# A second source-sorted table for 12 more pairs, and the first pairs dealt out in lots over layer one

## The chip, the cores and the metric

The kernel runs on one core of a Trainium2 chip. The metric is the device time of one launch in microseconds. The core has five engines that run their own instruction streams in order: TensorE (PE, with its weight loads shown as PEld), VectorE (DVE), ScalarE (ACT), GpSimd (POOL) and SyncE (SP). DMAs are issued by SP, ACT and POOL. POOL issues the indirect ones, in which every row has an address of its own.

## The reference, cut to what matters

Three layers of a relational graph network over N = 6250 nodes of D = 256 features and E = 100000 edges with R = 3 relations, all float32:

```python
ew = edge_attr @ edge_w + edge_b                      # (E, 256), the same in all layers
for l in range(3):
    msg = relu(x[src] * ew)                           # a row of x per edge
    out = 0
    for i in range(3):                                # relation i
        h = segment_sum(msg * (edge_type == i), dst) * inv_cnt[i]
        out = out + h @ weights[l, i]
    x = x + relu(out + x @ roots[l] + biases[l])
return layernorm(x0 + x)
```

The edges come sorted by `dst`, and `dst` is drawn as 6250 u², so that the low nodes have by far the most edges: the first 7168 edges all end in the first 40 nodes.

## The kernel before, in words

**Pairs and steps.** Edges are taken 128 at a time, one to a partition, and two such tiles are a pair: 391 pairs of 256 edges. A quad is two pairs (four tiles, 128x1024 elements). In every layer a list `order` says in which order the pairs are worked, and the loop over `it` is software-pipelined around it: at step `it` PE reduces pair `order[it]`, DVE multiplies (`weigh`) the quad of pair `order[it+3]`, PE makes the edge weights of `order[it+5]` (layer one; later layers load them back from `ew_all`), and POOL gathers pair `order[it+9]`. The steps only fix the order of each engine's own instructions; in time the engines run apart as far as data and buffers allow. Gathered rows sit in `xs`, which has 8 quad buffers, so that POOL can be some 16 pairs ahead of the reduction.

**A pair's work.** `gather_pair` (L1300) issues two indirect DMAs on POOL, 128 rows of x each. `weigh` multiplies a quad by its edge weights on DVE (L813) and applies relu on ACT (L814). `one_hot` builds four 128x120 selection tiles on DVE (L827: 3 relations by a window of 40 nodes). `reduce` multiplies rows by selections on PE into `h_p` (L844 or L852), and `add` puts the 40-node window of a span of pairs into the ring `acc` on DVE (L884, or L873 for the place of the first 40 nodes, which needs no address). When a block `c` of 128 nodes is complete (step `starts[c]`), `node_mul` multiplies it by the relation weights on PE (L913), `node_end` adds up on DVE (L944, L947) and SP stores the block to `x_mid` in DRAM (L950) for the next layer's gathers; in layer three DVE also does the layer norm of the block (L953 to L965, L1015). Blocks 1 to 48 end in order, 4 to 16 steps apart; block 0, where the most edges end, ends last.

**The zone.** The first Z = 28 pairs all end in the first 40 nodes. In layer one they are gathered like the others, 28 pairs in one run at steps 104 to 131, and `scatter` (L708) also writes each of their edge-weight rows with an indirect DMA on POOL into `zone_table` in DRAM, sorted by source: one scatter behind each gather, four to a quad. The place of each row in the table is counted out beforehand in layer one (`sort_begin`, `sort_hot`, `sort_count`, `sort_end`), and `sort_clear` blanks the table (L599). In layers two and three these 28 pairs are not gathered. Instead 25 *lots* of 2 pairs (one per 256 source nodes) stand in the order, one every 12 pairs (`ZONE_EVERY`): SP loads 512 table rows (L725), and since each of a lot's four tiles holds edges from one known half-block of 64 sources, the rows of x are made on chip: PE spreads the row numbers over the partitions (`seed_ew`, L753), DVE compares them with the partition number (`choose`, L769, 128x256), PE multiplies that by `x_all` in SBUF (`expand`, L777), and DVE weighs the result (L813, tile `zone`). No indirect DMA is issued for a lot.

**The end of a layer.** Pairs 51 down to 28 end in the first 128 nodes and come last in every layer; with them block 0 is complete. `gather_early` then issues the next layer's first 6 pairs (12 indirect DMAs from `x_mid`, tile index `src_e`), which read all blocks but block 0; what they lack of block 0 is added on chip (`complete`). It stands `SOON` = 3 steps before the end of the order. After that the gathers need block 0 in `x_mid`.

Of the kernel before, what the change touches and what calls it, by code (L numbers as in the profile page):

```python
# [442 lines left out]
def ordered_path(ctx, tc, x, attr_laid, A, weights, roots, biases, edge_w, edge_b, out, src, src_i, seg, place_i, consts, x_root,  # L443
# [6 lines left out]
    nc = tc.nc  # L450
# [12 lines left out]
    Z = zone_of(N, E)  # L463
    ZU = first_zone(N, E)
    slots = 2 * (ZU + 2 * -(-NT // 2) - ZU) * P
# [97 lines left out]

    zt = 2 * Z
# [14 lines left out]

    def sort_begin():  # L580
# [8 lines left out]
        nc.vector.tensor_scalar(slot_i, mine, P // 2 - 1, None, op0=ALU.bitwise_and)  # L589
        nc.vector.tensor_copy(meta[:, :, 0], seg[:, :zt])  # L590
# [11 lines left out]
    def sort_hot(g):  # L602
        hots[g] = early_pool.tile([P, 4, WK], BF, name="sort_hot")
        for i in range(4):
            t = 4 * g + i
            nc.vector.tensor_scalar(hots[g][:, i, :], iota_w[:, :, :WIN], slot_f[:, t:t + 1], None, op0=ALU.is_equal)
            if t == 0:
# [13 lines left out]
    def sort_end():  # L621
        most_p = o_pool.tile([P, 2, D], F32, name="o_p")
        crowd = early_pool.tile([P, 2], F32, name="crowd")
        nc.vector.tensor_reduce(crowd[:, 0:1], rank, AX.X, ALU.max)
        nc.vector.scalar_tensor_tensor(slot_f, slot_f, float(P), rank, op0=ALU.mult, op1=ALU.add)
# [37 lines left out]
    def layer(l, r_sb, b_sb, ats, early, pools):  # L663
# [5 lines left out]
        steps = len(order)  # L669
        taken, turns, added, banks = stages(N, E, share, l)  # L670
# [8 lines left out]
        r_next, ats_next, early_next = (None, None), {}, {}  # L679
        seen, h_bank, ew_ss, zone, hot, row_in, waiting = [0], {}, {}, {}, {}, {}, []  # L680
# [23 lines left out]
        def scatter():  # L704
            if waiting:
                there, q, k, i = waiting.pop(0)
# [60 lines left out]
        def choose(q):  # L767
            hot[q] = late_pool.tile([P, 2, P], F32, name="hot", bufs=2)
            nc.vector.tensor_scalar(hot[q].rearrange("p i e -> p (i e)"), ew_ps[q][:, 0, 0, :], half_i, None,  # L769
                                    op0=ALU.is_equal)  # L770

        def expand(q):
            c = 2 * (q - ZU // 2)
# [6 lines left out]
        def make_ew(q):  # L780

            n = len(pairs_of(q))
            at = ats[2 * q // GROUP, 2 * q < Z][:, q % (GROUP // 2), :]
# [85 lines left out]
        def add(span):  # L869
            u = span[0]  # L870
            if u < Z or u >= ZU:
# [115 lines left out]
        if l > 0:  # L987
            for p, u in enumerate(order):
                if u >= ZU:
                    assert all(p - 5 < starts[c] for c in (u - ZU, u - ZU + 1 - 2 * (u % 2)) if 0 < c < NT)  # L990
        for it in range(-11, max(starts) + 8):
            def pair(k):
# [3 lines left out]
            if l < L - 1 and 0 <= it + SOON - steps < FIRST:  # L996
                gather_early(it + SOON - steps)
# [5 lines left out]
            if l == 0 and pair(AHEAD) is not None and (pair(AHEAD) // GROUP, pair(AHEAD) < Z) not in ats:  # L1003
                ats[pair(AHEAD) // GROUP, pair(AHEAD) < Z] = load_at(pair(AHEAD) // GROUP)
# [80 lines left out]
            for span in add_at.get(it, ()):  # L1085
                add(span)
        return (*r_next, ats_next, early_next)
# [21 lines left out]
ROOTS = 24  # L1109
# [8 lines left out]
CLEARS = 20  # L1118
CLEAR_EVERY = 4
SORT_AT = 4  # L1120
SORT_EVERY = 5
ZONE_AT = 104
ZONE_FROM = 12
ZONE_EVERY = 12
# [4 lines left out]
def zone_of(N, E):  # L1129
# [7 lines left out]
    return v  # L1137

# [33 lines left out]
def zone_pairs(N, E):  # L1172

    ZU = first_zone(N, E)
    return [(ZU + 2 * j, ZU + 2 * j + 2) for j in range(-(-N // 256))]


def spans_in(N, E, l):

    spans = spans_of(N, E)  # L1180
    return spans if l == 0 else spans[1:] + zone_pairs(N, E)
# [15 lines left out]
def order_of(N, E, l):  # L1197
# [3 lines left out]
    Z = zone_of(N, E)  # L1201
# [4 lines left out]
    if l == 0:  # L1206
        at = where(K + ZONE_AT)
        order[at:at] = range(Z - 1, -1, -1)
    else:
        for j, (u, v) in enumerate(zone_pairs(N, E)):  # L1210
# [7 lines left out]
def stages(N, E, share, l):  # L1218

    order = order_of(N, E, l)  # L1220
    Z = zone_of(N, E)
# [257 lines left out]
```

## Time and profile before

| | |
|---|---|
| median of 3 runs | 2923.25 us (2922.34 to 2927.55) |
| profiled execution, its own time | 2919.59 us |
| its span | 2917.5 us |
| layer one on POOL, up to its last gather | 1064.2 us |
| layer two on POOL, last gather to last gather | 920.4 us |
| from layer two's last gather to the end | 932.9 us |
| busy: PE, DVE, ACT, POOL | 80%, 73%, 58%, 75% |
| indirect DMAs on POOL | 2234 gathers, 56 scatters |
| mean granted TensorE clock | 0.93 |

The profiled execution lies 3.7 us (0.13%) under the median. Busy times are of the engine itself; what its sequencer needs to issue a DMA is not in them, so that an engine that issues DMAs without a pause is shown under 100%.

### The profile page before, as it was taken

The numbers are of one execution on the slowest core, as the hardware profiler recorded it, in microseconds if no ns is written. First come the engines' busy times: TensorE is split into PE (matmuls) and PEld (weight loads), VectorE is DVE, ScalarE is ACT, GpSimd is POOL, SyncE is SP. The second block draws the span as 40 slices with busy tenths as digits, with TensorE's granted clock in tenths as the row PEclk, the third lists the DMA queues.
The fourth block names the chain that finished last, engine by engine and source line by source line (L and its number), as shares of the span: only waits on it lengthen the run. The fifth ranks groups of instructions, "written<-read, shape, count | busy, mean of one in ns | idle before, by whom it ended". The sixth has DMA issues, their size and how long they took to land.

```text
span 2917.5 us, 42955 instructions
## 1 busy us (share of the span) xinstructions
PE 2346.3 (80%) x12885; PEld 1799.7 (62%) x12885; DVE 2125.3 (73%) x5375; ACT 1694.0 (58%) x2153; POOL 2179.8 (75%) x2300
## 2 busy tenths in 40 slices
PE   5799768989999996778888888777677887877776
PEld 2456535667666765556667676665455666766665
DVE  7787424777777866666778788776577778988987
ACT  5678636877777765555555455444455554544554
POOL 7777777777777767777777777777777777777775
PEclk9999968999999998898999999989899998999999
DMA  7888536767767668677777777767777777777775
GB/s 236 307 306 289 175 123 202 226 219 234 236 219 240 228 225 264 222 231 233 241 228 235 228 240 241 238 215 246 223 242 230 233 247 231 244 241 231 249 246 174
DMA packets 275051, 679.64 MB, mean 233 GB/s; under 512 B 50986, under 2 KB 124732, under 8 KB 274812
## 3 DMA queue, kind: packets, MB, share of 16 engines
q1 hardware_dynamic: 157456, 368.21, 36.2%
q0 software_dynamic: 109920, 300.36, 34.2%
q10 hardware_dynamic: 7436, 8.24, 0.9%
q8 instruction: 106, 1.74, 0.2%
q14 instruction: 133, 1.09, 0.1%
HBM read 541.38 MB, written 135.23 MB: 232 GB/s over the span
## 4 chain that ended last, share of the span: by engine, by line
PE 25%; POOL 14%; DMA 13%; issue 12%; DVE 10%; ACT 2%; DVEq 1%; SPq 0%; ACTq 0%; POOLq 0%
POOL xs L1300 14%; DMA xs<-x_mid,src_r 11%; PE h_p L852 8%; PE o_p L913 7%; PE h_p L844 4%; DVE xs L813 3%; PE ew_p L791 3%; DVE oh L827 2%; DVE acc L884 1%; DVE x_root L944 1%; PE r_p L897 1%; PE ew_p L777 1%; ACT xs L814 1%; DMA ew_s<-ew_all 1%; PE r_p L889 1%
## 5 line engine op out<-in xcount | busy, mean ns | idle before, releaser
L1300 POOL DMA_INDIRECT xs<-x_mid,src_r x1428 | 1354.8, 949 | 437.9 <-issue 372.6
L814 ACT ACTIVATE xs<-xs 128x1024 f32<-128x1024 f32 (+1 forms) x557 | 585.0, 1050 | 792.0 <-DVE xs L813 770.3
L813 DVE TENSOR_TENSOR xs<-ew_p,xs 128x1024 f32<-128x1024 f32 (+1 forms) x557 | 675.6, 1213 | 381.8 <-DMA xs<-x_mid,src_r 195.7
L1300 POOL DMA_INDIRECT xs<-in_x_dram,src_io x770 | 733.6, 953 | 238.6 <-issue 194.9
L852 PE MATMUL h_p<-oh,xs 128*128 128x120 f32 x4848 | 685.2, 288 | 148.9 <-DVE acc L884 59.0
L852 PEld LDWEIGHTS h_p<-oh,xs 128*128 128x128 f32 x4848 | 635.3, 198 | 236.1 <-issue 93.6
L844 PE MATMUL h_p<-xs,oh 128*120 128x256 f32 x2020 | 594.5, 429 | 69.1 <-issue 20.7
L827 DVE TENSOR_SCALAR oh<-iota_w,seg_o 128x120 f32<-128x120 f32 x2234 | 593.2, 327 | 0.0
L913 PE MATMUL o_p<-w_sb,acc 128*128 128x256 f32 (+1 forms) x1752 | 468.2, 406 | 66.1 <-DVE x_root L944 61.7
L844 PEld LDWEIGHTS h_p<-xs,oh 128*120 128x120 f32 x2020 | 371.3, 203 | 202.6 <-issue 69.3
L884 DVE TENSOR_TENSOR acc<-h_p,acc 128x240 f32 (+1 forms) x741 | 327.2, 442 | 146.2 <-PE o_p L913 72.1
L913 PEld LDWEIGHTS o_p<-w_sb,acc 128*128 128x128 f32 (+1 forms) x1752 | 330.7, 200 | 151.8 <-DVE x_root L944 73.3
L758 ACT ACTIVATE ew_p<-ew_s 128x1024 f32<-128x1024 f32 x364 | 368.0, 1011 | 12.4 <-DMA ew_s<-ew_all 12.4
L791 PE MATMUL ew_p<-ew_sb,at 64*128 64x512 f32 x782 | 238.3, 686 | 66.9 <-ACT ew_p L761 59.8
L742 ACT ACTIVATE keep<-ew_p 128x1024 f32<-128x1024 f32 x182 | 185.4, 1019 | 118.4 <-issue 59.4
L944 DVE SCALAR_TENSOR_TENSOR x_root<-o_p,inv,x_root 128x256 f32<-128x256 f32 (+1 forms) x438 | 210.1, 480 | 41.5 <-PE o_p L913 34.6
L761 ACT ACTIVATE ew_p<-seed 128x1024 f32<-128x1024 f32 x194 | 198.4, 1023 | 0.0
L897 PE MATMUL r_p<-r_sb,t_s 128*128 128x256 f32 x588 | 168.0, 410 | 30.1 <-ACT t_s L893 30.0
L889 PE MATMUL r_p<-ident_o,x_all 128*128 128x128 f32 x294 | 67.8, 316 | 126.4 <-DVE x_root L900 126.1
L930 ACT ACTIVATE acc<-zero_o 128x768 f32<-128x768 f32 (+1 forms) x150 | 140.3, 936 | 20.5 <-PE o_p L913 20.4
L889 PEld LDWEIGHTS r_p<-ident_o,x_all 128*128 128x128 f32 x294 | 33.5, 150 | 187.8 <-DVE x_root L900 119.2
L897 PEld LDWEIGHTS r_p<-r_sb,t_s 128*128 128x128 f32 x588 | 107.5, 200 | 56.9 <-ACT t_s L893 40.4
(168 smaller groups left out, 1815.6 us busy)
## 6 DMA issues: line engine op xcount, KB each, us to landing
ew_s<-ew_all SPq DMA_DIRECT2D x362, 512.0 KB
ew_all<-keep SPq DMA_DIRECT2D x181, 512.0 KB
zone<-zone_table SPq DMA_DIRECT2D x50, 516.0 KB
xs<-x_mid,src_r POOLq DMA_INDIRECT x1428
zone_table<-blank SPq DMA_DIRECT2D x20, 645.0 KB
at<-in_attr_laid_dram SPq DMA_DIRECT2D x50, 256.0 KB
xs<-in_x_dram,src_io POOLq DMA_INDIRECT x770
x_mid<-x_all SPq DMA_DIRECT2D x96, 128.0 KB
```

The costliest lines, as they stand in the source:

```text
L758: nc.scalar.activation(ew_ps[q][:, :n], ew_ss[q][:, :n], AF.Copy)
L791: nc.tensor.matmul(ew_ps[q][:, k].rearrange("p i d -> p (i d)"), at[half, :], ew_sb[half].rearrange("p i d -> p (i d)"), start=False, stop ...
L813: nc.vector.tensor_mul(there, ew_ps[q][:, pairs.start:pairs.stop], there)
L814: nc.scalar.activation(there, there, AF.Relu)
L827: nc.vector.tensor_scalar(ohs[q][:, i, :], iota_w[:, :, :WIN], at, None, op0=ALU.is_equal)
L844: nc.tensor.matmul(h_p[:WK, :D], ohs[u // 2][:, t, :], rows_of(u, i), start=(i == 0 and first), stop=(i == 1 and closes(u)), skip_group_ch ...
L852: nc.tensor.matmul(h_p[:, d * WK:(d + 1) * WK], rows_of(u, i)[:, d * P:(d + 1) * P] if d < DC else full_ones, (ohs if d < DC else oh_bs)[u ...
L884: nc.vector.tensor_tensor(there, h_ps[span][:, :CH * WK].rearrange("p (c r w) -> p c r w", c=CH, r=R), there, op=ALU.add)
L897: nc.tensor.matmul(rs[c][:, 1, :], t_ss[c][:, d, :], r_sb[:, d, :], start=(d == 0), stop=(d == DC - 1))
L913: nc.tensor.matmul(o_p[:n, j, :], acc[:, d, r, slot:slot + n], w_sb[:, r * DC + d, :], start=(d == 0), stop=(d == DC - 1))
L944: nc.vector.scalar_tensor_tensor(root, o_p[:n, j, :], inv[:n, c, r:r + 1], root, op0=ALU.mult, op1=ALU.add)
L1300: nc.gpsimd.indirect_dma_start(out=xs[:, u % 2, i, :], out_offset=None, in_=x_rows[:, :], in_offset=bass.IndirectOffsetOnAxis(ap=src_i[:, ...
```

## The change

The next span, pairs 28 to 39, becomes part of the zone (`zones_end` gives 40, `zone_of` still 28). Its 12 pairs get a second part of the table, sorted by whole blocks of 128 sources, in 13 lots of 2 pairs (one per 512 sources, four tiles of one block each). Layer one keeps all gathers and issues 24 scatters more. Layers two and three lose the 12 pairs' gathers and edge-weight loads, and have 38 lots instead of 25, about one every 8 pairs; 21 of them stand behind pair 208, where 13 stood before. For a new lot PE spreads four 128x128 rows of numbers, DVE compares 128x512 elements, and PE expands with all 128 partitions. In layer one the zone's pairs no longer stand in one run: quads of them stand every 10 to 12 pairs from step 180 on, and the last six quads (pairs 11 to 0) right ahead of the last run, which is now 51 to 40. The table has 29696 rows instead of 19968 and is cleared in 30 DMAs instead of 20; the sort takes 20 groups instead of 14. The attribute load of a zone quad is one of its own (`load_one_at`). `gather_early` moves: `soon` is 3 after layer one as before, and -2 after layer two, 5 steps later, since block 48 starts at step 424 of 427 there (before: 398 of 413). `x_root` has 22 buffers instead of 24.

```diff
+    soon = min(SOON, steps - starts[NT - 1] - 5)
...
         def seed_ew(q):
...
+            if 2 * q >= Z2U:
+                for i in range(4):
+                    nc.tensor.matmul(ew_ps[q][:, 0].rearrange("p i d -> p (i d)")[:, i * P:(i + 1) * P],
+                                     row_in[q].rearrange("p k i -> p (k i)")[:, i:i + 1].to_broadcast([P, P]), ident_b,
+                                     start=(i == 0), stop=(i == 3), skip_group_check=True)
+                return
...
         def choose(q):
...
+            if 2 * q >= Z2U:
+                hot[q] = late_pool.tile([P, 4, P], F32, name="hot_4")
+                nc.vector.tensor_scalar(hot[q].rearrange("p i e -> p (i e)"), ew_ps[q][:, 0].rearrange("p i d -> p (i d)"),
+                                        node_i[:, 0:1], None, op0=ALU.is_equal)
+                return
...
         def expand(q):
...
+            if 2 * q >= Z2U:
+                c = 4 * (q - Z2U // 2)
+                for i in range(4):
+                    nc.tensor.matmul(ew_ps[q][:, i // 2, i % 2, :], hot[q][:, i, :], x_all[:, min(c + i, NT - 1), :],
+                                     start=(i % 2 == 0), stop=(i % 2 == 1), skip_group_check=True)
+                return
...
         def add(span):
-            u = span[0]
-            if u < Z or u >= ZU:
+            u = span[0] if span[0] < Z2U else Z1
+            if u < Z1 or u >= ZU:
...
-            if l < L - 1 and 0 <= it + SOON - steps < FIRST:
-                gather_early(it + SOON - steps)
+            if l < L - 1 and 0 <= it + soon - steps < FIRST:
+                gather_early(it + soon - steps)
...
-ROOTS = 24
+ROOTS = 22
...
-CLEARS = 20
+CLEARS = 30
...
-SORT_EVERY = 5
-ZONE_AT = 104
+SORT_EVERY = 6
+ZONE_AT = 168
+ZONE_SPACE = 11
+ZONE_LAST = 6
 ZONE_FROM = 12
-ZONE_EVERY = 12
+ZONE_EVERY = 8
...
+def zones_end(N, E):
+
+    return spans_of(N, E)[1][1]
...
     if l == 0:
-        at = where(K + ZONE_AT)
-        order[at:at] = range(Z - 1, -1, -1)
+        for j, u in enumerate(range(Z - 2, -1, -2)):
+            at = where(K + ZONE_AT + ZONE_SPACE * j) if K + ZONE_AT + ZONE_SPACE * j < U - 2 else order.index(U - 1) + 1 + 2 * j
+            if u < 2 * ZONE_LAST:
+                at = order.index(last - 1)
+            order[at:at] = (u + 1, u)
```

**POOL, layer one.** The program's order on POOL from the first gathers of layer one on; `zone_table<-keep,slot_i` is a scatter, `xs<-in_x_dram` a gather. Before:

```order
L1300 DMA xs<-in_x_dram,src_io 128x256 x225
L708 DMA zone_table<-keep,slot_i 19968x258
L1300 DMA xs<-in_x_dram,src_io 128x256
L708 DMA zone_table<-keep,slot_i 19968x258
L1300 DMA xs<-in_x_dram,src_io 128x256
```

Now:

```order
L1360 DMA xs<-in_x_dram,src_io 128x256 x353
L727 DMA zone_table<-keep,slot_i 29696x258
L1360 DMA xs<-in_x_dram,src_io 128x256
L727 DMA zone_table<-keep,slot_i 29696x258
L1360 DMA xs<-in_x_dram,src_io 128x256
L727 DMA zone_table<-keep,slot_i 29696x258
L1360 DMA xs<-in_x_dram,src_io 128x256
L727 DMA zone_table<-keep,slot_i 29696x258
L1360 DMA xs<-in_x_dram,src_io 128x256 x25
```

Before, 56 scatters and gathers alternate in one stretch behind the 225th gather of this row; now groups of four scatters come from the 353rd on, with 21 to 25 gathers between them, and the last six groups stand together near the end of the layer.

**DVE, the end of layer two.** The program's order on DVE from layer two's last products (`xs<-ew_p` 128x256 x2) to layer three's first. The operands `o_p,inv,x_root` are a node block's sums, `x_all<-x_root` ends the block (106 partitions: block 48; the one with `r_p` in it: block 0), and `xs<-o_p` is `complete`. Before:

```order
L819 TENSOR_TENSOR xs<-ew_p,xs 128x256 x2
L877 TENSOR_LOAD place_i
L884 ISA
L884 TENSOR_TENSOR acc<-h_p,acc 128x6x40
L944 SCALAR_TENSOR_TENSOR x_root<-o_p,inv,x_root 128x256
L944 SCALAR_TENSOR_TENSOR x_root<-r_p,inv,x_root 128x256
L944 SCALAR_TENSOR_TENSOR x_root<-o_p,inv,x_root 128x256
L947 SCALAR_TENSOR_TENSOR x_all<-x_root,x_all 128x256
L808 TENSOR_TENSOR xs<-o_p,xs 128x512
```

Now:

```order
L855 TENSOR_TENSOR xs<-ew_p,xs 128x256 x2
L963 TENSOR_TENSOR acc<-acc 128x6x40
L980 SCALAR_TENSOR_TENSOR x_root<-o_p,inv,x_root 128x256 x2
L983 SCALAR_TENSOR_TENSOR x_all<-x_root,x_all 128x256
L980 SCALAR_TENSOR_TENSOR x_root<-o_p,inv,x_root 106x256
L913 TENSOR_LOAD place_i
L920 ISA
L920 TENSOR_TENSOR acc<-h_p,acc 128x6x40
L980 SCALAR_TENSOR_TENSOR x_root<-o_p,inv,x_root 106x256 x2
L983 SCALAR_TENSOR_TENSOR x_all<-x_root,x_all 106x256
L980 SCALAR_TENSOR_TENSOR x_root<-o_p,inv,x_root 128x256
L980 SCALAR_TENSOR_TENSOR x_root<-r_p,inv,x_root 128x256
```

Before, only block 0 was left behind the last products; now blocks 47 and 48 end there too, and the early gathers of layer three, which read block 48, come after it.

**DVE, a lot in layer three.** The program's order on DVE from the comparison of a lot (`hot`) to its selections (`oh<-iota_w,zone`). Before, in the first half of the layer:

```order
L769 TENSOR_SCALAR hot<-ew_p,half_i 128x256
L900 TENSOR_TENSOR x_root<-r_p,b_sb 128x256
L827 TENSOR_SCALAR oh<-iota_w,seg_o 128x120 x4
L813 TENSOR_TENSOR zone<-ew_p,zone 128x4x256
L827 TENSOR_SCALAR oh<-iota_w,zone 128x120 x4
```

Now, one of the 13 new lots, late in the layer:

```order
L795 TENSOR_SCALAR hot_24031<-ew_p,node_i 128x512
L920 ISA
L920 TENSOR_TENSOR acc<-h_p,acc 128x6x40
L863 TENSOR_SCALAR oh<-iota_w,seg_o 128x120 x4
L920 ISA
L920 TENSOR_TENSOR acc<-h_p,acc 128x6x40
L849 TENSOR_TENSOR zone<-ew_p,zone 128x4x256
L980 SCALAR_TENSOR_TENSOR x_root<-o_p,inv,x_root 128x256
L920 ISA
L920 TENSOR_TENSOR acc<-h_p,acc 128x6x40
L863 TENSOR_SCALAR oh<-iota_w,zone 128x120 x4
```

The lot's own instructions are the same but for the comparison, which is twice as wide; 26 more of them stand on DVE in layers two and three together, and one more `add` for each.

More of the change, by code (lines that the diff above doesn't have):

```diff
@@ L989, in layer @@
                 if u >= ZU:
[L990 removed]
+                    u -= u % 2
+                    blocks = range(u - ZU, u - ZU + 2) if u < Z2U else range(2 * (u - Z2U), 2 * (u - Z2U) + 4)
+                    assert all(p - 4 < starts[c] for c in blocks if 0 < c < NT), (u, p)
         for it in range(-11, max(starts) + 8):
+            it_is[0] = it
             def pair(k):
@@ L1086, in layer @@
                 add(span)
+        assert not waiting
         return (*r_next, ats_next, early_next)
```

47 lines of the change are left out of this document (35 added, 12 removed).

## The prediction

> **What bounds the kernel now.** I read the page's head, POOL's waits, and its groups by line.
>
> ```profile
> span 2917.5 us, 42955 instructions
> PE 2346.3 (80%) x12885; PEld 1799.7 (62%) x12885; DVE 2125.3 (73%) x5375; ACT 1694.0 (58%) x2153; POOL 2179.8 (75%) x2300
> POOL xs L1300 <- issue: 573.9, 1884, 0.3
> ...
> L1300 POOL DMA_INDIRECT xs<-x_mid,src_r x1428 | 1354.8, 949 | 437.9 <-issue 372.6 <-DMA xs<-x_mid,src_r 17.1 <-PE h_p L844 7.6
> L1300 POOL DMA_INDIRECT xs<-in_x_dram,src_io x770 | 733.6, 953 | 238.6 <-issue 194.9 <-DMA xs<-in_x_dram,src_io 8.2 <-ACT ew_p L761 6.5
> L708 POOL DMA_INDIRECT zone_table<-keep,slot_i x56 | 54.8, 979 | 18.0 <-issue 14.6 <-ACT keep L736 1.3 <-DMA zone_table<-keep,slot_i 0.9
> ```
>
> No engine shows over 80%, but POOL's 75% is a full engine: a gather is busy for 0.95 us and then idle for 0.30 us, nearly always on "issue", which is its own sequencer (573.9 us in 1884 pieces of 0.3). So a gather costs 1.25 us and a scatter 1.28 us, and the 2290 of them make 2290 x 1.25 = 2863 of the 2917.5 us. Whether POOL also sets the pace is told by who waits for its rows. These are DVE's waits in layer two (1500 to 1900 us), then the first and the second half of layer three (2000 to 2400, 2400 to 2850):
>
> ```profile
> DVE xs L813 <- DMA xs<-x_mid,src_r: 28.4, 15, 5.0
> ```
>
> ```profile
> DVE xs L813 <- DMA xs<-x_mid,src_r: 77.8, 30, 5.2
> ```
>
> ```profile
> DVE acc L884 <- PE o_p L913: 17.9, 11, 3.5
> DVE mv L964 <- ACT mv L959: 12.6, 13, 1.3
> DVE zone L813 <- PE ew_p L777: 11.4, 10, 2.1
> DVE x_root L944 <- PE o_p L913: 4.3, 9, 0.9
> ...
> DVE xs L813 <- DMA xs<-x_mid,src_r: 1.0, 1, 1.0
> ```
>
> Early in layer three DVE waits 77.8 of 400 us for gathered rows: POOL paces it. From 2400 us on it waits 1.0 us for them: DVE, with the PE and ACT waits of its own instructions, is the pace, and POOL runs ahead into the free buffers. Layer two lies between, with 28.4 of 400 us to spare. The stages, with PE, PEld, DVE, ACT and POOL busy, the granted clock and the DMA share (zone run of layer one, its later part, layer two, the two halves of layer three):
>
> ```profile
> 300.00:440.00 140.00, 97.67 (x380) 59.70 (x378) 49.31 (x127) 63.61 (x82) 105.83 (x109) 0.78 0.44 139
> 600.00:1000.00 400.00, 377.88 (x2400) 280.73 (x2398) 305.99 (x735) 302.20 (x361) 302.82 (x320) 0.99 0.69 228
> 1500.00:1900.00 400.00, 319.94 (x2005) 278.29 (x2006) 317.06 (x798) 203.14 (x238) 302.56 (x320) 0.94 0.74 238
> 2000.00:2400.00 400.00, 299.79 (x1369) 228.88 (x1369) 281.15 (x697) 212.92 (x296) 302.85 (x320) 0.91 0.74 241
> 2400.00:2850.00 450.00, 349.86 (x2197) 302.33 (x2196) 392.22 (x1031) 228.43 (x292) 340.90 (x359) 0.95 0.75 242
> ```
>
> In the last row DVE is busy for 392.2 of 450 us, and the waits above add 46 us: nothing is left over. So an indirect DMA saved is worth its 1.25 us in layers one and two, and nothing behind 2400 us, where only DVE's work counts.
>
> **Layer one: +30.8 us.** All its gathers stay, and 24 scatters at 0.979 + 0.30 = 1.28 us come on a POOL that has no pause: +30.8 us. The 24 more sort groups' parts on DVE and PE, the 10 clearing DMAs and the small attribute loads on SP lie beside POOL: in the zone run DVE is busy for 49 of 140 us and the DMA engines for 44%, and later DVE for 306 of 400. If that cover failed, POOL would run out of buffers; in layer one PE, busy for 378 of 400 us, would be the first to show it. Spreading the zone removes no POOL instruction.
>
> **Hand-over to layer two: -11.5 us.** POOL's rows at the end of layer one, and of layer two:
>
> ```profile
> 1063.23 0.94 POOL L1300 DMA_INDIRECT xs<-in_x_dram,src_io  x1 [0.30 <-issue]
> 1073.05 0.95 POOL L1300 DMA_INDIRECT xs<-x_mid,src_e  x1 [8.88 <-DMA ew_all<-keep]
> ...
> 1090.93 0.94 POOL L1300 DMA_INDIRECT xs<-x_mid,src_r  x1 [3.18 <-PE o_p L806]
> ```
>
> ```profile
> 1983.67 0.95 POOL L1300 DMA_INDIRECT xs<-x_mid,src_r  x1 [0.30 <-issue]
> 1984.92 0.95 POOL L1300 DMA_INDIRECT xs<-x_mid,src_e  x1 [0.30 <-DMA xs<-x_mid,src_r]
> ...
> 1999.94 0.94 POOL L1300 DMA_INDIRECT xs<-x_mid,src_r  x1 [0.30 <-issue]
> ```
>
> From the end of the last gather to the next layer's first full one POOL needs 1090.93 - 1064.17 = 26.8 us after layer one and 1999.94 - 1984.62 = 15.3 us after layer two; 12 early gathers alone are 15.0. The difference is the lag of the other engines behind POOL: layer one ends PE-heavy (94%), so block 48 and block 0 are late. Now the last six zone quads stand there with their scatters, 24 x 1.28 = 31 us in which POOL is slower and PE is not asked for more, as in the zone run, where PE was at 70%. The gain lies between 0 and 11.5 us; I take 11.5, since 31 us are more than the whole lag.
>
> **Layer two: -30.0 us.** 24 gathers at 1.25 us fall away. What comes: in 400 us POOL gathers 160 pairs, which held 13.3 lots and now hold 20. A lot on DVE, by the starts of the next instruction (row_in, `hot`, product, `add`, selections):
>
> ```profile
> 2017.17 0.16 DVE L765 CAST row_in<-zone 128x4 bf16<-128x4 f32 x1
> 2017.24 1.06 DVE L827 TENSOR_SCALAR oh<-iota_w,seg_o 128x120 f32<-128x120 f32 x4
> 2018.23 1.21 DVE L813 TENSOR_TENSOR xs<-ew_p,xs 128x1024 f32<-128x1024 f32 x1
> 2019.36 0.47 DVE L769 TENSOR_SCALAR hot<-ew_p,half_i 128x256 f32<-128x256 f32 x1
> 2019.75 1.06 DVE L827 TENSOR_SCALAR oh<-iota_w,seg_o 128x120 f32<-128x120 f32 x4
> 2021.09 1.23 DVE L813 TENSOR_TENSOR zone<-ew_p,zone 128x1024 f32<-128x1024 f32 x1 [0.28 <-PE ew_p L777]
> 2022.23 0.40 DVE L884 TENSOR_TENSOR acc<-h_p,acc 128x240 f32 x1
> 2022.54 1.06 DVE L827 TENSOR_SCALAR oh<-iota_w,zone 128x120 f32<-128x120 f32 x4
> 2023.52 1.21 DVE L813 TENSOR_TENSOR xs<-ew_p,xs 128x1024 f32<-128x1024 f32 x1
> ...
> L808 DVE TENSOR_TENSOR xs<-o_p,xs 128x512 f32<-128x512 f32 x2 | 1.4, 686 | 1.0 <-PE o_p L806 1.0
> ```
>
> 0.07 + 0.39 + 1.14 + 0.31 + 0.98 = 2.9 us, and 11.4 / 10 = 1.1 us of waiting for the expansion: 4.0 us. The new comparison of 128x512 has no row; it lies between one and two of the old (0.39 to 0.78). The nearest row reads 128x512 from PSUM in 0.69 us of duration, 0.21 more than the 0.47 of `hot`, so a new lot takes 4.2 us. In the Trainium skill, the page "VectorE: DVE Perf Modes" (section "The TRN2 errata — SBUF-src ops pay a fixed extra latency per instruction") gives a PSUM read 120 cycles and one per element at 0.96 GHz, an estimate of 0.66 us for it and 0.39 for the old one; no run here shows the wide one, and by that figure the sum would be 0.4 us higher.
>
> So 6.7 lots more are 27 us per 400, against 28.4 us of waiting for rows: they fit, barely, and POOL keeps the pace. On PE the stage has 80 of 400 us idle for them.
>
> **Hand-over to layer three: +11.5 us.** Before, block 48 had long been stored when layer two's last gather was issued. Now it ends behind the layer's last `add`, and the early gathers wait for it. Rows of that place before (the last `add`, block 0's last step, its store):
>
> ```profile
> 1992.36 0.41 DVE L884 TENSOR_TENSOR acc<-h_p,acc 128x240 f32 x1 [3.42 <-PE h_p L852]
> ...
> 1996.24 0.42 DVE L947 SCALAR_TENSOR_TENSOR x_all<-x_root,x_all 128x256 f32<-128x256 f32 x1
> 1996.69 0.33 SPq L950 DMA_DIRECT2D x_mid<-x_all  x1
> ```
>
> The last `add` starts 7.7 us behind POOL's last gather; block 48 needs two sums and its last step (0.41 + 2 x 0.5), so its store goes out at about 9.5. Block 0's store at 1996.69 released gathers at 1999.94 at the latest, 3.3 us; with 2 to 3.3 us for landing the early gathers start at 11.5 to 12.8 and end 15 us later, 11.2 to 12.5 us behind the 15.3 of before. I take 11.5. On POOL everything of layer three queues behind them.
>
> **Layer three: +20.4 us.** Up to 2400 us POOL paces, and 5 lots more at 4.2 us go into 77.8 us of waiting: nothing. Behind pair 208, which is about there, 21 lots stand instead of 13, 7 of the 8 being new: 8 x 4.0 + 7 x 0.21 = +33.5 us. The last run has 6 quads fewer: 6 x (1.13 + 0.98) = -12.7, and one `add` less, -0.3. The sum is +20.4 us; the 30 us of gathers that POOL saves do not show. Without the waits for expansion it would be +11.7; with twice these, +29.
>
> **Sum.** 30.8 - 11.5 - 30.0 + 11.5 + 20.4 = +21.2 us against the profiled 2919.6 us, which lies 3.7 us under the median. On the median of 2923.25 that is 2944 us, 0.7% slower.
>
> **Rivals.**
> (a) Faster: DVE sheds its waits, so that POOL paces layer three to its end. Then its 24 gathers count too, and the sum is 21.2 - 20.4 - 30 = -29 us, 2894. For this the 46 us of waits behind 2400 us would have to go, since the last row of the stages leaves DVE no other room and it gets 12 us of its own work more. Nothing in the trace speaks for that.
> (b) PE runs at a higher clock. In the trace the clock was 0.78 where PE was busy for 70%, 0.99 at 94%, and 0.95 in the DVE-paced stage at 78%. With the lots' work there the stage might reach 0.99: 350 us of PE become 336, and if all 14 us come off DVE's waits the sum is +7 us, 2930. In the Trainium skill, the page "TensorE: Matmul & The Clock Gate" (section "What's actually happening") has the throttled state as the default that activity lifts; by that rule more lots pay for part of themselves, and the trace's stages agree in direction (0.78 against 0.99).
> (c) Layer two falls behind as layer one did. A lot on PE (reduction, expansion, spread numbers, 25 lots):
>
> ```profile
> L844 PE MATMUL h_p<-zone,oh 128*120 128x256 f32 x200 | 52.0, 394 | 6.6 <-DVE acc L884 4.0 <-DMA ew_s<-ew_all 2.0 <-PE h_p L852 0.6
> L777 PE MATMUL ew_p<-x_all,hot 64*128 64x256 f32 x200 | 32.0, 441 | 5.5 <-DVE hot L769 5.5
> L753 PE MATMUL ew_p<-ident_b,row_in 128*64 128x128 bf16 x100 | 8.1, 244 | 0.7 <-DVE row_in L765 0.7
> ```
>
> That is 92.1 / 25 = 3.7 us; a new one expands with all 128 rows, at most as dear as the reduction, 4.5 us. 6.7 lots more take PE to some 347 of 400 us (87%) and DVE to 337 (84%) at once; layer one at 94% of PE lagged 11.5 us at its end. That would come on the hand-over, and the waits for expansion may double (+9): 2953 to 2966.
> (d) The spread zone does not shorten the hand-over to layer two: +11.5 us, 2956.
>
> **How the numbers follow.** The forecast (2930 to 2952) has 0.47, (a) 0.08, (b) 0.15, (c) and (d) together 0.30. From no change 0.2% (5.8 us) is about what a measurement of this kernel can tell. Faster: (a) and a little of (b), 0.11. Within: most of (b), 0.13. Slower: 0.76. The range leaves out (a) and the worst of (c): 2922 to 2966. Where only "slower" counts, the forecast's own bounds are the +11.7 and +29 of layer three.
>
> **What would show it.** Right: 80 scatters without pauses on POOL in layer one and its last gather some 31 us later; a hand-over near 15 us; layer two's last-to-last gather time (920.4 us) some 42 us shorter; then a pause of POOL of about 10 us ahead of the `src_e` gathers; behind layer three's middle no DVE waits for `xs`, and POOL waiting for buffers, not for issue. Wrong: DVE waiting for `xs` late in layer three (a), a clock of 0.99 there (b), or POOL idle in the middle of layer two (c).

## The result and the profile after

| | before | after |
|---|---|---|
| median of 5 runs | 2922.34 us (2919.91 to 2927.55) | 2960.64 us (2958.67 to 2966.95) |
| ratio, 95% interval | | 1.013 (1.0117 to 1.0144) |
| profiled execution, its span | 2919.59, 2917.5 us | 2958.67, 2956.9 us |

The changed kernel is 1.3% slower, 38 us where 21 were forecast. Its median lies inside the stated range (2922 to 2966 us) but above the forecast's own bounds (2930 to 2952). The page of after, its head and its gathers of layers two and three:

```profile
span 2956.9 us, 44413 instructions
PE 2431.0 (82%) x13409; PEld 1878.4 (64%) x13409; DVE 2211.6 (75%) x5620; ACT 1712.6 (58%) x2203; POOL 2157.4 (73%) x2276
...
L1360 POOL DMA_INDIRECT xs<-x_mid,src_r x1380 | 1309.5, 949 | 458.4 <-issue 362.8
```

48 gathers fewer in these layers and 24 scatters more in layer one leave POOL with 22 us less work, and PE and DVE with 85 us each more. POOL's timeline (start, duration, idle time before and what ended it) at the first scatter, at the end of layer one and at the end of layer two:

```profile
474.45 0.94 POOL L1360 DMA_INDIRECT xs<-in_x_dram,src_io  x1 [0.30 <-issue]
485.70 0.99 POOL L727 DMA_INDIRECT zone_table<-keep,slot_i  x1 [10.31 <-ACT keep L755]
...
1101.85 0.95 POOL L1360 DMA_INDIRECT xs<-in_x_dram,src_io  x1 [0.30 <-PE h_p L888]
1103.10 0.95 POOL L1360 DMA_INDIRECT xs<-x_mid,src_e  x1 [0.30 <-issue]
...
1121.18 0.95 POOL L1360 DMA_INDIRECT xs<-x_mid,src_r  x1 [3.40 <-PE r_p L842]
...
1984.26 0.94 POOL L1360 DMA_INDIRECT xs<-x_mid,src_r  x1 [0.30 <-issue]
2001.60 0.95 POOL L1360 DMA_INDIRECT xs<-x_mid,src_e  x1 [16.40 <-PE o_p L842]
...
2016.61 0.95 POOL L1360 DMA_INDIRECT xs<-x_mid,src_r  x1 [0.30 <-issue]
```

The first scatter of the kernel before, for comparison:

```profile
318.21 0.99 POOL L708 DMA_INDIRECT zone_table<-keep,slot_i  x1 [1.25 <-ACT keep L736]
```

From these rows come the stages, cut as the prediction cut them (the end of a layer's last gather; the start of the next layer's first full gather):

| stage, us | before | after | change | predicted |
|---|---|---|---|---|
| layer one to its last gather | 1064.2 | 1102.8 | +38.6 | +30.8 |
| hand-over to layer two | 26.8 | 18.4 | -8.4 | -11.5 |
| layer two | 893.7 | 864.0 | -29.7 | -30.0 |
| hand-over to layer three | 15.3 | 31.4 | +16.1 | +11.5 |
| layer three to the end | 917.5 | 940.3 | +22.7 | +20.4 |
| span | 2917.5 | 2956.9 | +39.4 | +21.2 |

All five signs and the order of the sizes are as forecast. The largest miss is layer one. The one new wait there is the 10.31 us in the second row above (1.25 us before), which no part of the prediction mentions.

DVE's and POOL's longest waits in layer three from 2450 to 2850 us (total, times, longest), first DVE, then POOL:

```profile
DVE acc L920 <- PE o_p L949: 19.2, 10, 5.0
DVE mv L1000 <- ACT mv L995: 9.0, 10, 1.2
DVE zone L849 <- PE ew_p L813: 8.9, 6, 2.3
```

```profile
POOL xs L1360 <- issue: 81.5, 244, 1.8
POOL xs L1360 <- ACT xs L850: 14.3, 10, 5.2
POOL xs L1360 <- ACT ew_p L783: 8.5, 8, 3.8
```

DVE has no row that waits for gathered rows; POOL waits for its buffers, which come free behind DVE's products (`ACT xs`). Its last gather ends 40.0 us before the span does; before it was 22.0 us. The same stretch in the stages view, of before and of after (PE, PEld, DVE, ACT and POOL busy, granted clock, DMA share, GB/s):

```profile
2450.00:2850.00 400.00, 307.61 (x1945) 264.93 (x1944) 352.49 (x930) 204.84 (x262) 303.09 (x319) 0.97 0.75 242
```

```profile
2450.00:2850.00 400.00, 317.53 (x1926) 275.79 (x1927) 338.19 (x885) 194.38 (x247) 282.07 (x297) 0.93 0.72 232
```

Before, POOL still issued 319 DMAs in these 400 us, its full rate (one per 1.25 us). After, it issued 297: it no longer set the pace.

### The profile page after: what moved, and what is told of

It is laid out like the page before. It is cut to its first block, busy times and chain, and to the rows that moved or that the text cites. A ratio compares the mean times of both kernels' runs of the same rounds, so it can differ in the third digit from the quotient of the medians.

```text
span 2956.9 us, 44413 instructions
## 1 busy us (share of the span) xinstructions
PE 2431.0 (82%) x13409; PEld 1878.4 (64%) x13409; DVE 2211.6 (75%) x5620; ACT 1712.6 (58%) x2203; POOL 2157.4 (73%) x2276
## 5 line engine op out<-in xcount | busy, mean ns | idle before, releaser
L1360 POOL DMA_INDIRECT xs<-x_mid,src_r x1380 | 1309.5, 949 | 458.4 <-issue 362.8
L850 ACT ACTIVATE xs<-xs 128x1024 f32<-128x1024 f32 (+1 forms) x545 | 572.3, 1050 | 671.3 <-DVE xs L849 646.8
L849 DVE TENSOR_TENSOR xs<-ew_p,xs 128x1024 f32<-128x1024 f32 (+1 forms) x545 | 661.0, 1213 | 343.3 <-ACT keep L761 171.3
L880 PE MATMUL h_p<-xs,oh 128*120 128x256 f32 x1972 | 562.5, 416 | 64.2 <-issue 16.1
L880 PEld LDWEIGHTS h_p<-xs,oh 128*120 128x120 f32 x1972 | 351.1, 197 | 186.0 <-issue 41.4
L920 DVE TENSOR_TENSOR acc<-h_p,acc 128x240 f32 (+1 forms) x773 | 340.6, 441 | 149.4 <-PE o_p L949 63.7
L827 PE MATMUL ew_p<-ew_sb,at 64*128 64x512 f32 x702 | 216.4, 693 | 27.2 <-ACT ew_p L786 16.1
L850 ACT ACTIVATE zone<-zone 128x1024 f32<-128x1024 f32 x76 | 80.5, 1059 | 231.5 <-DVE zone L849 207.6
L880 PE MATMUL h_p<-zone,oh 128*120 128x256 f32 x608 | 156.4, 389 | 26.8 <-DVE acc L920 21.0
L849 DVE TENSOR_TENSOR zone<-ew_p,zone 128x1024 f32<-128x1024 f32 x76 | 92.9, 1223 | 97.0 <-PE ew_p L813 52.3
```

What stands on the lines that cost most here:

```text
L827: nc.tensor.matmul(ew_ps[q][:, k].rearrange("p i d -> p (i d)"), at[half, :], ew_sb[half].rearrange("p i d -> p (i d)"), start=False, stop ...
L849: nc.vector.tensor_mul(there, ew_ps[q][:, pairs.start:pairs.stop], there)
L850: nc.scalar.activation(there, there, AF.Relu)
L880: nc.tensor.matmul(h_p[:WK, :D], ohs[u // 2][:, t, :], rows_of(u, i), start=(i == 0 and first), stop=(i == 1 and closes(u)), skip_group_ch ...
L920: nc.vector.tensor_tensor(there, h_ps[span][:, :CH * WK].rearrange("p (c r w) -> p c r w", c=CH, r=R), there, op=ALU.add)
L1360: nc.gpsimd.indirect_dma_start(out=xs[:, u % 2, i, :], out_offset=None, in_=x_rows[:, :], in_offset=bass.IndirectOffsetOnAxis(ap=src_i[:, ...
```

## The experiments

Stages of each kernel in us, as above, from its POOL timeline, with its median and its ratio to the kernel before on the same chip. One profiled execution stands for a kernel, and equal stages scatter. Layer three without edits to it took 917 to 927 us with the old lots and 940 to 947 us with the new ones. Layer one of the kernel before took 1064.2 us and, in `nonorm_before_2`, 1071.3; that of the changed kernel took 1102.8, 1103.4 (`nonorm_after_2`) and 1101.8 (`l3_old`, which also stores six more quads there).

| kernel | median | ratio (95%) | layer one | hand-over | layer two | hand-over | layer three |
|---|---|---|---|---|---|---|---|
| `spread_only` | 2913.6 | 0.9976 (0.9967 to 0.9986) | 1063.0 | 15.3 | 894.4 | 15.5 | 927.4 |
| `second_only` | 2992.7 | 1.0237 (1.0221 to 1.0253) | 1104.8 | 47.4 | 866.3 | 32.0 | 944.5 |
| `zone_earlier` | 2973.0 | 1.0170 (1.0154 to 1.0185) | 1113.5 | 18.5 | 866.4 | 31.4 | 947.4 |
| `l3_old` | 2944.6 | 1.0077 (1.0059 to 1.0095) | 1101.8 | 20.3 | 863.3 | 31.4 | 925.9 |
| `sooner_and_free` | 2948.3 | 1.0084 (1.0069 to 1.0100) | 1101.2 | 18.6 | 864.6 | 19.0 | 946.3 |
| `spread_normact` | 2910.5 | 0.9957 (0.9943 to 0.9971) | 1067.9 | 15.3 | 894.3 | 15.4 | 915.8 |
| `nonorm_after_2` | 2912.1 | 0.9958 (0.9941 to 0.9974) | 1103.4 | 16.8 | 865.5 | 31.7 | 888.9 |
| `nonorm_before_2` | 2919.1 | 0.9983 (0.9973 to 0.9992) | 1071.3 | 27.5 | 896.8 | 15.6 | 912.2 |

### The two halves of the change

**`spread_only`**: the changed kernel without a second table, the old 28 pairs in lots.

```diff
 def zones_end(N, E):
-    return spans_of(N, E)[1][1]
+    return zone_of(N, E)
...
 def zone_pairs(N, E):
-    return [(ZU + 2 * j, ZU + 2 * j + 2) for j in range(halves + blocks)]
+    return [(ZU + 2 * j, ZU + 2 * j + 2) for j in range(halves)]
...
-CLEARS = 30
+CLEARS = 20
...
-SORT_EVERY = 6
-ZONE_AT = 168
-ZONE_SPACE = 11
+SORT_EVERY = 5
+ZONE_AT = 112
+ZONE_SPACE = 26
...
-ZONE_EVERY = 8
+ZONE_EVERY = 12
```

> The kernel before with the zone's 14 lots of two pairs spread over layer one (eight alone, six together ahead of the last 20 pairs); no second table. No DMA more or less on POOL. Theory (the hand-over to layer two is the other engines' lag behind POOL, and scatters late in the layer let them catch up): the lead of POOL over the weighing at the layer's last gather falls from 12.6 us to about 4.5 us, the hand-over from 26.8 to about 18.4 us, the time by 8 to 11 us against the kernel before: 2911 to 2914 us, ratio 0.996 to 0.997. Rival (a lag given up in layer one comes back as a stall there or in layer two): within 3 us of the kernel before.

POOL at the end of its layer one:

```profile
1062.06 0.94 POOL L1360 DMA_INDIRECT xs<-in_x_dram,src_io  x1 [0.30 <-DMA xs<-in_x_dram,src_io]
1063.30 0.94 POOL L1360 DMA_INDIRECT xs<-x_mid,src_e  x1 [0.30 <-issue]
...
1077.07 0.94 POOL L1360 DMA_INDIRECT xs<-x_mid,src_e  x1 [0.30 <-issue]
1078.31 0.95 POOL L1360 DMA_INDIRECT xs<-x_mid,src_r  x1 [0.30 <-issue]
```

No row waits: the hand-over is the 12 early gathers alone, 15.3 us instead of 26.8, less than the 18.4 expected, and the time falls by 8 us. The theory holds; rival (d) of the prediction falls. This half of the change beats the kernel before.

**`second_only`**: the changed kernel with all 40 pairs in one run.

```diff
-            at = where(K + ZONE_AT + ZONE_SPACE * j) if K + ZONE_AT + ZONE_SPACE * j < U - 2 else order.index(U - 1) + 1 + 2 * j
-            if u < 2 * ZONE_LAST:
-                at = order.index(last - 1)
+            at = where(K + ZONE_AT) + 2 * j
```

> The changed kernel with its zone of 40 pairs in one run at step 180 of layer one, instead of in lots spread over it. Theory: layer one up to its last gather stays some 31 to 39 us over that of before; after the run the lag of the other engines grows again as before, to 12 us at the last gather, so the hand-over to layer two is back near 26 us and the time is 8 us over the changed kernel, 2966 to 2971 us (ratio to the kernel before 1.016). Rival (the spreading is worth nothing): 2960 us, ratio 1.013.

It lost 32 us against the changed kernel, not 8. POOL, the end of its layer one, and DVE, the last step of block 48 (106 partitions):

```profile
1103.60 1.20 POOL L1358 DMA_INDIRECT xs<-in_x_dram,src_io  x1 [0.30 <-issue]
1137.16 0.95 POOL L1358 DMA_INDIRECT xs<-x_mid,src_e  x1 [32.37 <-ACT acc L966]
```

```profile
1131.84 0.43 DVE L983 SCALAR_TENSOR_TENSOR x_all<-x_root,x_all 106x256 f32<-106x256 f32 x1
```

Without lots behind the last edges block 48 starts at step 388 of 391, so `soon` is -2 here too, and the early gathers wait for that block, as they do after layer two: in both places the first of them starts 4.9 us behind the end of block 48's last step (here 1132.27 us), though the rows name other engines. On top of it the other engines lag by 14.8 us, where the changed kernel has 4.5. So the lots at the end do two things: they let the engines catch up, and they give block 48 time to be stored. The expectation saw the first alone.

### Layer one's stall

Lead is the time from the end of a quad's last gather on POOL to the start of its product on DVE:

| layer one, lead in us | step 96 | step 138 | step 168 | step 180 | first scatter waits |
|---|---|---|---|---|---|
| after | 12.1 | 14.4 | 19.4 | 23.8 | 10.31 |
| `second_only` | 12.6 | 13.4 | 17.7 | 22.5 | 9.00 |
| `sooner_and_free` | 13.4 | 18.9 | 16.2 | 18.7 | 5.23 |

In each row the wait is the lead at step 180 less 13.5 us, and so it is in `l3_old` (22.5 and 9.03) and `nonorm_after_2` (21.2 and 7.78). A scatter stands in POOL's order only four to five pairs, 2.5 us each, behind the last gather of its quad, and what it writes must have passed PE and ACT (`keep`): a POOL that leads by more than 13.5 us stands still there, and everything behind the scatter with it. The 13.5 us are those of step 180. In the kernel before, whose zone run stands at steps 116 to 143 (not 104 to 131), the first scatter waits 1.25 us at a lead of 12.3; in `spread_only`, at step 124, it waits 0.30 us at a lead of 11.1.

**`zone_earlier`**: first lot at step 124, sort groups every 4 pairs.

```diff
-SORT_EVERY = 6
-ZONE_AT = 168
-ZONE_SPACE = 11
+SORT_EVERY = 4
+ZONE_AT = 112
+ZONE_SPACE = 15
```

> The changed kernel with the first spread lot at step 124 of layer one instead of 180 (lots 15 pairs apart, the sort's groups every 4 pairs). At step 124 POOL leads the weighing by 13 to 15 us, at step 180 by 23.8. Theory (the 10.3 us stall at 485.70 us is the first scatter, which stands in POOL's order only ten pairs behind the gather of its rows, so that a POOL that leads by more than about 17 us waits for the kept rows): the stall falls to 0 to 3 us, layer one's last gather ends near 1093 to 1095 us instead of 1102.8, the time falls by 7 to 10 us against the changed kernel: 2950 to 2954 us. Rival (the other engines lag by as much all the same, and the stall returns at a later scatter or at the hand-over): 2960 us, no change.

A miss with the wrong sign: 12 us slower than the changed kernel. The expectation also had the distance wrong: ten pairs and 17 us, where it is four to five pairs and 13.5 us. ACT, SP and POOL there:

```profile
349.58 1.03 ACT L755 ACTIVATE keep<-ew_p 128x1024 f32<-128x1024 f32 x1 [0.70 <-PE ew_p L827]
```

```profile
345.59 0.43 SPq L613 DMA_DIRECT2D zone_table<-blank  x1
```

```profile
340.08 0.95 POOL L1360 DMA_INDIRECT xs<-in_x_dram,src_io  x1 [0.30 <-ACT keep L761]
354.26 1.00 POOL L727 DMA_INDIRECT zone_table<-keep,slot_i  x1 [13.23 <-ACT xs L850]
```

The lead at step 126 is 20.8 us, where the changed kernel has 16.0 and `spread_only`, whose sort ended at step 88, has 11.0: the denser sort made the engines lag more. By the 13.5 us of step 180 that would be a wait of 7.3 us, not of 13.23. The scatter starts 3.7 us behind the end of its `keep`; the last clearing DMA had been issued only 8.7 us before it, and probably that is what it waited for, but no row shows it. Another wait of POOL, at 103 us, took 8.43 us, where the executions with a group every 6 pairs have 2.12 to 4.48.

**`sooner_and_free`**: the sort every 5 pairs with the lots where they were; and the early gathers of layer three freed.

```diff
-SORT_EVERY = 6
+SORT_EVERY = 5
...
-        soon = min(SOON, steps - starts[NT - 1] - 5)
+        soon = SOON
...
-            gather_pair(nc, early_next[u // 2], x_mid[l][:N, :], src_e, u, order[0])
+            gather_pair(nc, early_next[u // 2], x_mid[0][:N, :], src_e, u, order[0])
```

> The changed kernel with two edits that lie in different stages and are read apart in the trace. First, the sort's groups come every 5 pairs instead of 6, so that the sort is done at step 139 instead of 170, 41 steps ahead of the first spread lot. Theory 1 (the sort's parts on DVE and PE make these engines lag behind POOL while they run, 12 us at step 96 and 23.8 at step 180 in the changed kernel, and the first scatter collects the lag as its 10.3 us stall): lead of 12 to 17 us at step 180, a first scatter that waits 0 to 3 us, layer one's last gather at 1093 to 1096 us instead of 1102.8, 7 to 10 us won. Rival 1 (a denser sort only lags more and the lag stays): stall of 10 us or more. Second, the early gathers of layer three are freed from layer two's last block: issued three pairs earlier and reading the rows that layer one stored (the first six pairs of layer three have the values of layer one; nothing else is left out). Theory 2 (the 16.4 us pause is the wait for block 48, and POOL paces what comes next): the hand-over to layer three is 15 to 16 us instead of 31.4, and layer three is no longer than before, 935 to 945 us. Rival 2 (DVE paces layer three from its beginning): the hand-over is short, but layer three grows by 10 us or more. Both theories right: 2935 to 2941 us; theory 1 alone: 2950 to 2954; theory 2 alone: 2944 to 2948; neither: about 2960 us.

```profile
483.36 1.00 POOL L727 DMA_INDIRECT zone_table<-keep,slot_i  x1 [5.23 <-ACT keep L755]
...
1984.69 0.95 POOL L1360 DMA_INDIRECT xs<-x_mid,src_e  x1 [0.30 <-issue]
...
1998.60 0.95 POOL L1360 DMA_INDIRECT xs<-x_mid,src_e  x1 [0.30 <-issue]
2003.38 0.94 POOL L1360 DMA_INDIRECT xs<-x_mid,src_r  x1 [3.84 <-PE o_p L842]
```

First edit: the stall halves, but the lead falls only to 18.7 us, where 12 to 17 were expected. Layer one ends just 1.6 us earlier: of the 5.1 us won there 2.2 are lost again in POOL's waits near 105 and 116 us, and 1.2 in DMAs that took a little longer. That is no clear gain: executions with the changed kernel's layer one are themselves 1.6 us apart, and their waits near 105 us differ by 2.4.

A denser sort does go with a larger lag while it runs: at step 96 the lead is 11.9 to 12.8 us with a group every 6 pairs (four executions), 13.3 to 14.3 with one every 5 (five), and 17.0 with one every 4. `spread_only`, with 14 groups that end at step 88 and its first scatter at step 124, has no scatter that waits even 1 us (2.72 us is the longest in `spread_normact`, which has the same layer one); no kernel here with 20 groups is without the stall.

Second edit: the pause of 16.4 us is gone. Layer three, 946.3 us, is 6.0 us longer than the changed kernel's, but no longer than in the other kernels with the new lots (940.3 to 947.4). The time is 12 us under the changed kernel, as expected of theory 2 alone (2944 to 2948 us); rival 2 is not borne out. The hand-over stays at 19.0 instead of 15.3 us, because now block 0 is waited for (3.84 us in the last row).

### Layer three

**`l3_old`**: second table in layer two alone.

```diff
-    spans = [s for s in spans_of(N, E) if s[0] >= ZE]
-    return ... + spans if l == 0 else spans + zone_pairs(N, E)
+    spans = [s for s in spans_of(N, E) if s[0] >= (ZE if l < 2 else zone_of(N, E))]
+    return ... + spans if l == 0 else spans + (zone_pairs(N, E) if l < 2 else zone_pairs(N, E)[:-(-N // 256)])
...
+                if 2 * q >= Z1:
+                    nc.sync.dma_start(ew_all[q]..., there...[:, :, :D])
```

> The changed kernel with the second table used in layer two alone; layer three gathers pairs 28 to 39 and has the 25 old lots, 12 pairs apart; for this the edge terms of six more quads are stored in layer one by SP. Theory (layer three is paced by DVE behind its middle, where a gather saved is worth nothing and a new lot costs 4 us): layer three from its first full gather to the end falls from 940.3 us to the 917.6 us of before, the time by some 23 us to about 2938 us, although 24 gathers more are issued there. Rival 1 (POOL is the pace of layer three after all): 30 us of gathers come back, time 2960 to 2990 us. Rival 2 (layer three's length is something else, the clock or the new order of spans): less than 8 us of change, 2953 to 2960 us.

2944.6 us, 16 us under the changed kernel, and layer three 14.4 us shorter, though it issues 24 gathers (30 us) more. Rival 1 is out, and rival 2, which allowed less than 8 us, too. It came back to 925.9, not to 917.6; `spread_only`, whose layer three is that of before, shows 927.4. The late stretch of `l3_old`:

```profile
2450.00:2850.00 400.00, 310.90 (x1911) 267.61 (x1910) 340.56 (x892) 197.71 (x252) 300.30 (x316) 0.93 0.74 237
```

The granted clock is 0.93 as in the changed kernel, so that the clock does not make the difference between the two.

**`nonorm_after_2`, `nonorm_before_2`**: both kernels without layer three's norm.

```diff
-            stats = edge.tile([P, nc.vector.BN_STATS_DIM], F32, name="stats")
-            nc.vector.bn_stats(stats[:n], x_all[:n, c, :])
-            mv = mvs[c] = edge.tile([P, nc.vector.BN_AGGR_DIM + 1], F32, name="mv")
-            nc.vector.bn_aggr(mv[:n, :nc.vector.BN_AGGR_DIM], stats[:n])
+            nc.sync.dma_start(out[c * P:c * P + n, :], x_all[:n, c, :])
...
-                deviate(node_at[it - 5])
+                pass
...
-                norm(node_at[it - 6])
+                pass
```

> The changed kernel without the layer norm of the 49 blocks in layer three (left out: statistics, reciprocal and scaling on DVE, square root on ACT; the blocks are stored as they are). By the changed kernel's rows DVE is spared 0.43 + 0.18 + 0.16 + 0.42 us of work and 0.41 us of waiting per block, some 60 us in the layer, 35 to 40 of it behind 2450 us. Theory (DVE, with the waits of its own instructions, is the pace of layer three behind its middle): layer three from its first full gather to the end falls from 940 to 895 to 908 us, POOL's pauses behind 2600 us go, the time falls by 35 to 50 us, to 2911 to 2926 us. Rival (PE at its granted clock of 0.92 is the pace and DVE waits for it anyway; the small gain of the scaling moved to ACT speaks for it): less than 15 us, over 2945 us. Between the two: both engines wait for each other in turn, and the gain is the share that DVE has.

> The kernel before without the layer norm of layer three (the same parts left out). Theory (POOL issues there without a pause to its last gather, and only the 22 us behind it hold a lag of DVE, 5 us of which the last blocks need in any case): the time falls by 8 to 14 us, to 2908 to 2914 us, and the difference between the changed kernel and the kernel before shrinks from 38 us to between 0 and 15 us. Rival (PE is the pace): both fall by less than 12 us and the difference stays over 30 us.

```profile
2450.00:2850.00 400.00, 332.47 (x2118) 287.95 (x2118) 342.27 (x867) 208.29 (x244) 303.13 (x319) 0.97 0.77 251
```

```profile
DVE xs L813 <- DMA xs<-x_mid,src_r: 26.2, 15, 4.7
DVE acc L884 <- PE o_p L913: 19.6, 10, 4.8
```

The changed kernel gains 48.6 us by losing 53 us of DVE's work (2211.6 to 2158.2 us busy) and 20 us of its waiting for the square root on ACT; the first fence is its late stretch: 319 DMAs again, POOL at its full rate, and the clock at 0.97 while PE does more. The kernel before loses as much of DVE's work (2125.3 to 2072.8) and gains 6 us; the second fence is its DVE in the same stretch, now waiting for rows: POOL had been its pace nearly to the end. With DVE relieved in both, the changed kernel is the faster one by 7 us, and its layer three is shorter by 23.3 us: up to the last gather by 30.6, the price of the 24 saved gathers, less a tail behind it that is 7.3 us longer. This is the decisive test: DVE takes the gain away.

The difference of the two kernels was expected to shrink to between 0 and 15 us, and it turned round. The expected 8 to 14 us of the kernel before were too many: its tail behind the last gather falls from 22.0 to 15.0 us although DVE has caught up, so that the last blocks need 15 us and not 5.

**`spread_normact`**: `spread_only` with the norm's scaling on ACT.

```diff
-            nc.vector.tensor_scalar(x_all[:n, c, :], x_all[:n, c, :], mv[:n, 0:1], mv[:n, 1:2],
-                                    op0=ALU.subtract, op1=ALU.mult)
+            nc.vector.tensor_scalar(mv[:n, 2:3], mv[:n, 0:1], mv[:n, 1:2], -1.0, op0=ALU.mult, op1=ALU.mult)
+            nc.scalar.activation(x_all[:n, c, :], x_all[:n, c, :], AF.Identity, bias=mv[:n, 2:3], scale=mv[:n, 1:2])
...
-                norm(node_at[it - 6])
+                norm(node_at[it - 7])
```

> The kernel with the spread zone alone (2913.6 us), and with the layer norm's scaling of 128x256 on ACT instead of DVE, one pair later, so that DVE does not wait for ACT's square root; DVE gets one operation of 128x1 more. By the rows of the changed kernel DVE is spared 0.42 + 0.41 - 0.16 = 0.67 us per block, 33 us in layer three and some 18 us behind 2400 us. Theory (behind the middle of layer three DVE is the pace, POOL runs ahead, and the 23.5 us between the last gather and the end are DVE's lag): the tail falls to 10 to 16 us, the time by 7 to 13 us against the spread zone alone: 2900 to 2907 us, ratio to the kernel before 0.992 to 0.995. Rival (PE at its granted clock is the pace there, and DVE waits for it anyway): tail of 20 us or more, 2911 to 2915 us.

2910.5 us, the fastest complete kernel here, 0.43% under the kernel before. Against `spread_only` it is 3 us, and the two intervals overlap; the tail fell from 23.5 to 20.1 us, not to 16. By its numbers the run lies with the rival (a tail of 20 us or more, 2911 to 2915 us) and does not speak for the theory. That PE is the reason is not shown: with old lots there is little lag of DVE to win, as `nonorm_before_2` shows.

### Four runs without a verdict

`sort_sooner` (3769.3 us), `early_free` (3779.8), the first `nonorm_after` (3750.2) and `nonorm_before` (3605.3) ran on a chip on which the kernel before itself took 3618.5 us. They hold the two edits of `sooner_and_free`, one each, and the two kernels without norm, and were expected to do the same as in the runs above; their ratios to the kernel before there were 1.043, 1.044, 1.039 and 0.996. POOL's longest wait in `nonorm_before` on that chip:

```profile
POOL xs L1297 <- issue: 1000.8, 2013, 6.3
```

The same kernel as `nonorm_before_2` has 568.8 us in pieces of at most 2.1. With POOL held up where it waits for nothing that the profile shows, POOL's pace, on which every expectation rests, is not given there, and nothing is drawn from these four.

## Why the prediction was right, and where not

**The range.** The measured 2960.6 us lies where the prediction had put its rivals (c) and (d), 2953 to 2966 us, and neither of them came. The five stages went the way that was forecast, and their sizes missed by 18 us in all, each to the slow side. That the range held all the same is in part luck.

**Layer two (-30.0, measured -29.7).** 690 gathers at 1.25 us are 862.5 us, and the stage took 864.0: POOL kept the pace with 38 lots, and rival (c) did not come. The bound for the unseen 128x512 comparison held: it takes 0.74 us, and the next instruction starts 0.66 us behind it (0.60 was assumed).

```profile
2045.20 0.74 DVE L795 TENSOR_SCALAR hot<-ew_p,node_i 128x512 f32<-128x512 f32 x1
2045.86 0.41 DVE L936 TENSOR_TENSOR x_root<-r_p,b_sb 128x256 f32<-128x256 f32 x1
```

In the Trainium skill, the page "VectorE: DVE Perf Modes" (section "The TRN2 errata — SBUF-src ops pay a fixed extra latency per instruction") gives a PSUM read 120 cycles and one per element at 0.96 GHz, an estimate of 0.66 us. The trace agrees: the two starts above lie 0.66 us apart.

**Layer three (+20.4, measured +22.7).** Mechanism and size hold: the mean over the kernels with new lots (940.3, 944.5, 947.4, 946.3) less that with old ones (917.5, 927.4, 925.9) is +21 us; the terms of the prediction's sum add up to 20.5. `nonorm_after_2` shows that it is DVE, and that rival (a) is what happens once DVE is relieved. One reading was too strong. In the kernel before DVE's 392.2 us and its 46 us of waits leave some 11 of the 450 us, not nothing, and POOL issues without a pause to its last gather: `nonorm_before_2` wins only 6 us, so that DVE and POOL were nearly even there.

**Layer one (+30.8, measured +38.6): the mis-sized term.** The step that failed is "the 24 more sort groups' parts on DVE and PE ... lie beside POOL". They lie beside it only as long as POOL waits for nobody. The first scatter, the first DMA in POOL's order that writes results of PE and ACT, met a lead of 23.8 us and collected 10.31 us. The 24 scatters with their gaps cost 31 us, as forecast; the stall's 10.0 us over a normal gap, less 2.5 us by which other waits and the gathers were shorter, make up the rest. The prediction looked for a POOL that runs out of buffers, and read DVE's and PE's shares; it had not asked which DMA of POOL waits for their results.

The stall stands in every execution of this layer one (7.78 to 10.31 us), but what it costs is less sure: with 7.78 us the layer took 1103.4 us, with 5.23 us 1101.2. And against the 1071.3 us that the old layer one took in `nonorm_before_2` the three executions of the changed one are 30.5 to 32.1 us longer, as forecast. So 7 us of the miss may be scatter.

That a denser sort makes the lag grow is shown above. The sort is not its only source: in the kernel before the lead grows from 2.0 us at step 182 to 16.1 at step 340, with no sort there and PE busy for 378 of 400 us. So a first scatter at step 180, after a long stretch without scatters, may have met a lag without the longer sort. That was not run apart, nor was a change that keeps 80 scatters and has no stall.

**Hand-over to layer two (-11.5, measured -8.4).** `spread_only` gives the forecast to the tenth. In the changed kernel the early gathers start at once, too, but the first full gather waits 3.40 us, for block 0, whose store SP issues at 1118.76 us. The other engines lag by 4.5 us at the end of layer one there, by 0.2 in `spread_only`.

**Hand-over to layer three (+11.5, measured +16.1).** The wait for block 48 is the cause, as `sooner_and_free` shows. The size was off at both ends. DVE, with block 48's last steps (106 partitions):

```profile
1993.46 0.41 DVE L920 TENSOR_TENSOR acc<-h_p,acc 128x240 f32 x1 [1.29 <-PE h_p L888]
1995.19 1.00 DVE L980 SCALAR_TENSOR_TENSOR x_root<-o_p,inv,x_root 106x256 f32<-106x256 f32 x2 [1.32 <-PE o_p L949]
1996.23 0.43 DVE L983 SCALAR_TENSOR_TENSOR x_all<-x_root,x_all 106x256 f32<-106x256 f32 x1
```

The last step ends at 1996.66, 11.5 us behind POOL's last gather, where the prediction had 9.5 for the store: the last `add` starts 0.6 us later than assumed, and between it and the block's sums DVE waits 1.32 us for PE, which the sum left out. And from there to the early gather at 2001.60 it is 4.9 us, not 2 to 3.3.

**Rival (b)** did not come: late in layer three the clock was 0.93 against 0.97 before, with PE busier. It rose to 0.97 when DVE was relieved in the changed kernel, and was 0.93 instead of 0.97 when DVE was relieved in the kernel before; whether it is cause or effect there stays open. It does not explain the longer layer three: with the old lots `spread_only` has 0.91 in this stretch and `l3_old` 0.93, and layer three takes 927.4 and 925.9 us there.

## What to carry to other kernels

Saving work on the engine that sets the pace is worth its price only in the stages where it does: ask for each stage who comes next and by how many microseconds, here 0 of 30 us in layer three. Work placed "beside" a busy queue that runs in order is free only until that queue first needs a result from the engines that do it; look for that instruction, and compare the queue's lead there with the distance it allows. And when a loop is lengthened, check what the planner puts at its end: block 48 being late cost 16 us after layer two and 32 us in `second_only`.
